# Plain products for the output projection and the values of an attention kernel with seven-product tricks, on one core

## The chip, the cores and the metric

The kernel runs on one core of one Trainium2 chip, all in float32 (the small feed-forward part in a split float32 form). The metric is the device time of one execution in microseconds, lower is better. The engines are named as in the profile: PE is TensorE's matmul, PEld its weight load, DVE VectorE, ACT ScalarE, POOL GpSimd, SP SyncE. SP, ACT and POOL also issue DMA transfers.

## The reference

`x` is 2048 x 256, there are 16 heads of 128, and a feed-forward of width 704 with weights rounded to -1, 0 and 1.

```python
xn = _layernorm(x, axis=-1)
# attention
qkv = einsum('bsd,ed->bse', xn, Wqkv).reshape(B, S, 3 * H, D)
q, k, v = qkv[:, :, :H], qkv[:, :, H:2*H], qkv[:, :, 2*H:]
w = softmax(einsum('bqhd,bkhd->bhqk', q, k) * D ** -0.5, axis=-1)
attn = einsum('bhqk,bkhd->bqhd', w, v).reshape(B, S, H * D)
attn = einsum('bse,de->bsd', attn, Wout)
# feed-forward on the same xn, weights quantized by their mean magnitude
ffn = bitlinear(sigmoid(bitlinear(xn, w1)) * bitlinear(xn, w2), w3)
return x + attn + ffn
```

## The kernel before, in words

**Blocks, tiles, groups.** After a lead-in (normalization, the feed-forward, the first head's Q, K and V) the kernel runs 64 blocks: 16 heads by 4 blocks of 512 queries. Two heads make a group (`G = 2`), so a group has 8 blocks, called block 0 to 7 of the group below; the last group is handled apart. A block has 4 tiles of 128 queries. The main loop has one step `u` per tile; the order of all instructions is written out by hand, and each engine takes its own in that order. `n` and `t` are the block and tile of the step.

**One step.** PE computes the scores of the tile six steps ahead (`scores`, `LEAD = 6`): 128 queries by 2048 keys, in two halves of 1024, out of three PSUM buffers. DVE takes the maximum of each half (`mx`, L630) and the negated one of both (`nm`, L633); ACT takes the exponential into `p` (L640), with the sums of rows. `exchanged` sends `p` to `part` by 16 transfers of 64 KB (L659), ten issued by SP and six by ACT: 32-row bands change places. Two steps later DVE turns `part` in 32x32 blocks into a slot of `R` (`transposed`, L706); now keys lie on partitions. The weighted sum of values is done by seven half-size products in place of eight (a Strassen-Winograd scheme over two halves of keys and two of head columns). It needs differences of `R` slots, taken by POOL (`differences`, L726: T1a and T3a in tile 3 of the block before; T1b, T3b and half of T2, called T2l, in tile 0; T2h and T4 in tile 1), and sums of V, taken by POOL once a head (`v_combined`, L748, two in tile 3 and two in tile 0 of a head's first block, which is block 0 or 4). `weighted` (L773) are these products, into `av`. Tile 1 needs T1, then T2l for its first half and T2h for its second. ACT copies and DVE adds quarters of `av` into `oU` (`copied` L791, `added` L799).

**The end of a block.** `inverses` (tile 2) makes 1/sum for the next block: a reduction, a reciprocal and a 32x32 turn on DVE, then four POOL-issued transfers of 4 x 32 numbers to DRAM (`rds`, L678). `spread` (tile 1 of that block) brings them back, the same on all partitions, into `oT` (L685). After tile 3 DVE multiplies `oU` by `oT` into `oT` (L801) and `put_away` sends `oT` to DRAM (`ods`, L827) at the start of the next block.

**Side products.** Each step also carries products that prepare other heads, through one PSUM bank `m` (`ps_m`, one buffer). `product(..., False)` runs right behind the scores; DVE reads its result behind `nm`; a second one (`twice`) follows the weighted products of the step, when the first has been read, and DVE reads it at the start of the next step (`left`). All are seven-product schemes, in 128x128x512 products cut into two 64-column halves (`in_halves`):
- tiles 2 and 3: Q and K of the next head, read by `fast_read`; in even blocks DVE also scales `kT` into `qT` (`fast_scaled`, L223), at the start of tile 3, and the first read of tile 3 (L197) needs that.
- tiles 0 and 1 of blocks 0 to 3: output projection of the group before (`fast_o_product`, `fast_o_read` L911), 7 products for two blocks, out of fetched pieces `o3` and their differences (POOL, L842), added into `osums`; running sums go to and from DRAM (`y_moved`, L839).
- tiles 0 and 1 of blocks 4 to 7: V of the next group (`fast_v_product`, `fast_v_read` L308 and L315), 7 products for half of the tokens. They give V with head columns on partitions, so it is sent to DRAM by bands (`v_sent`, L322), fetched (`v_landed`, L326) and turned by DVE (`v_transposed`, L331).

`between(n, t)` places all the POOL-issued transfers and sums at the end of a step. `weights[g, "v"]` and `weights[g, "o"]` share a buffer; their sums for the schemes (`sums_of`, L272 to L275) are POOL's.

Of the kernel before, what the change touches and what calls it, by code (L numbers as in the profile page):

```python
# [20 lines left out]
def layernorm_attention_bitffn_kernel(  # L21
# [197 lines left out]
    def fast_scaled(h: int, b: int):  # L219
        c = b // 2 * 2  # L220
        k1 = kTs[h].rearrange("p (j k r) -> p k j r", j=P // 32, r=32)[:, (c + 1) * TB : (c + 2) * TB]
        q0 = qTs[h, c].rearrange("p (k j r) -> p k j r", j=P // 32, r=32)
        nc.vector.tensor_scalar(q0, k1, SCALE, None, ALU.mult)  # L223
# [4 lines left out]
    o3 = const.tile([P, 3, QB], F32, tag="o3", name="o3")  # L228
# [36 lines left out]
    def v_sums(g: int):  # L265
        wv = weights[g, "v"]
        sums_of(wv[:, :, D:], wv[:, :, :D], f"wvs{g}")

    def sums_of(k, q, name: str):

        w = wpool.tile([P, 4, D], F32, tag="wx", name=name)
        nc.gpsimd.tensor_tensor(w[:, 0], q[:, 0], q[:, 1], ALU.add)  # L272
        nc.gpsimd.tensor_tensor(w[:, 1], w[:, 0], k[:, 0], ALU.subtract)
        nc.gpsimd.tensor_tensor(w[:, 2], k[:, 0], q[:, 0], ALU.subtract)
        nc.gpsimd.tensor_tensor(w[:, 3], k[:, 1], w[:, 1], ALU.subtract)  # L275
        wxs[name] = w


    def fast_v_product(g: int, m: int, second: bool):
        half, m = divmod(m, NB)  # L280
        wv, w, t = weights[g, "v"], wxs[f"wvs{g}"], ts[2 * half]
        x00, x10 = (xnT[:, d, bass.ts(2 * half, QB)] for d in range(KC))
        x11 = xnT[:, 1, bass.ts(2 * half + 1, QB)]
        lhs, rhs = (
            ((wv[:, 0, D:], x00), (w[:, 1], t[:, 1])),
            ((w[:, 2], t[:, 2]), (wv[:, 1, :D], t[:, 3])),
            ((w[:, 0], t[:, 0]), (w[:, 3], x11)),
            ((wv[:, 1, D:], x10),),
        )[m][second]
        pm = ps_m.tile([P, QB], F32, tag="m", name=f"pvw{g}_{half}_{m}_{int(second)}")  # L290
        in_halves(pm, lhs, rhs, True, True)
        return pm

    def v_half(h: int, half: int):
        return v_tile(h)[:, half * NKT // 2 : (half + 1) * NKT // 2]

    def fast_v_read(g: int, m: int, second: bool, pm):
        half, m = divmod(m, NB)
        q, k = (
            v_half(g * G + i, half).rearrange("p k d -> p (k d)").rearrange(  # L300
                "p (j k r) -> p k j r", j=P // 32, r=32
            )
            for i in range(G)
        )
        k0, k1, q0, q1 = k[:, :TB], k[:, TB:], q[:, :TB], q[:, TB:]
        pm = pm.rearrange("p (k j r) -> p k j r", j=P // 32, r=32)
        if (m, second) == (0, False):
            nc.vector.tensor_copy(k0, pm)  # L308
            return
        todo = {  # L310
            (0, True): ((k1, k0),), (1, False): ((q1, k1),), (1, True): ((q0, q1),),
            (2, False): ((q1, q1), (k1, k1)), (2, True): ((k1, k1),), (3, False): ((k0, k0),),
        }[m, second]
        for o, i in todo:
            nc.vector.tensor_tensor(o, pm, i, ALU.add)  # L315

    def v_sent(h: int, half: int):

        v = v_half(h, half).rearrange("p k d -> p (k d)")
        vd = vds[half].rearrange("(j r) (q c) -> q r j c", r=32, c=S // 8)  # L320
        for q in range(P // 32):
            nc.gpsimd.dma_start(vd[q], v[bass.ts(q, 32)].rearrange("r (j c) -> r j c", c=S // 8))  # L322

    def v_landed(half: int):
        for u in range(2):
            nc.gpsimd.dma_start(v_part[u], vds[half][:, bass.ts(u, QB)])  # L326

    def v_transposed(h: int, half: int):
        v = v_half(h, half).rearrange("p k (q r) -> p q k r", r=32)
        for u in range(2):  # L330
            nc.vector.transpose(  # L331
                v[:, 2 * u : 2 * u + 2], v_part[u].rearrange("p (q k r) -> p q k r", q=2, r=32)
            )

    wxs, v_part = {}, [xnT[:, 0, bass.ts(c, QB)] for c in (1, 3)]

# [11 lines left out]
        [away.tile([P, QB], F32, tag=f"od{h}_{c}", name=f"od{h}_{c}") for c in range(NB)]  # L348
        for h in range(2 * G)
    ]  # L350
    vds = [away.tile([P, S // 2], F32, tag=f"vd{i}", name=f"vd{i}") for i in range(2)]
    rds = [away.tile([TB, P], F32, tag=f"rd{i}", name=f"rd{i}") for i in range(2)]
# [311 lines left out]
    def inverses(n: int):  # L664
# [12 lines left out]
        for j in range(P // 32):  # L677
            nc.gpsimd.dma_start(  # L678
                rds[n % 2][:, bass.ts(j, 32)], riT[32 * j : 32 * j + TB, :]
            )  # L680

    def spread(n: int):

        if n < NBK - NB:
            nc.gpsimd.dma_start(oT, rds[n % 2].rearrange("t p -> (t p)").partition_broadcast(P))  # L685
            rbs[n] = oT
# [106 lines left out]
    def added(n: int, r: int):  # L793
# [6 lines left out]
        if r == 3 and n < NBK - NB:  # L800
            nc.vector.tensor_tensor(oT, u, rbs[n], ALU.mult)  # L801
# [22 lines left out]
    def put_away(n: int):  # L824

        h, b = blocks[n]
        nc.gpsimd.dma_start(ods[h % (2 * G)][b], oT)  # L827
# [6 lines left out]
    def o_fetched(g: int, pair: int, i: int, head: int, c: int):  # L834
        nc.gpsimd.dma_start(o3[:, i], ods[(g * G + head) % (2 * G)][2 * pair + c])

    def y_moved(pair: int, c: int, back: bool):
        y, yd = osums[:, c], yds[2 * pair + c]
        nc.gpsimd.dma_start(*((yd, y) if back else (y, yd)))  # L839

    def o_difference(i: int, a: int, b: int):
        nc.gpsimd.tensor_tensor(o3[:, i], o3[:, a], o3[:, b], ALU.subtract)  # L842

    def o_loaded(g: int, i: int):
        if i % 2 == 0:
            y_moved(i // 2, 0, False)

    def o_moved(g: int, i: int, t: int):

        pair, more = i // 2, i == 1  # L850
        at = i % 2, t
        if at == (0, 0):
            o_difference(1, 2, 1)
        elif at == (0, 1):
            o_difference(0, 1, 0)
        elif at == (0, 2):
            o_fetched(g, pair, 2, 1, 0)
        elif at == (1, 0):
            o_difference(2, 2, 1)
            if more:  # L860
                o_fetched(g, 1, 0, 0, 0)
        elif at == (1, 1):
            y_moved(pair, 1, True)
        elif at == (1, 2):
            if more:
                y_moved(1, 1, False)
                o_fetched(g, 1, 1, 0, 1)
            else:
                y_moved(pair, 0, True)
        elif at == (1, 3) and more:  # L870
            y_moved(pair, 0, True)
            o_fetched(g, 1, 2, 1, 1)
            o_difference(1, 1, 0)

    def o_begun(g: int, i: int, t: int):

        at = i, t
        if at == (6, 2):
            o_fetched(g, 0, 0, 0, 0)
        elif at == (6, 3):  # L880
            o_fetched(g, 0, 1, 0, 1)
        elif at == (7, 1):
            o_difference(1, 1, 0)
        elif at == (7, 2):
            o_fetched(g, 0, 2, 1, 1)

        if at == ((6, 3) if g else (7, 2)):
            y_moved(0, 1, False)

    def o_parts(g: int, m: int):  # L890
        w = weights[g, "o"]
        k, q = w[:, :, :P], w[:, :, P:]
        s = wxs[f"wos{g}"]
        k0, k1, q0, q1 = (0, 0), (1, 0), (0, 1), (1, 1)
        return (
            ((s[:, 0], 1, (k1, q1)), (s[:, 3], 2, (k1,))),
            ((k[:, 0], 0, (k1, q1, k0, q0)),),
            ((s[:, 2], 0, (q0, q1)), (k[:, 1], 2, (k0,))),
            ((s[:, 1], 1, (k1, q0, q1)), (q[:, 1], 2, (q0,))),
        )[m % NB]  # L900

    def fast_o_product(g: int, m: int, second: bool):
        lhs, i, _ = o_parts(g, m)[second]
        pm = ps_m.tile([P, QB], F32, tag="m", name=f"pow{g}_{m}_{int(second)}")
        in_halves(pm, lhs, o3[:, i], True, True)
        return pm

    def fast_o_read(g: int, m: int, second: bool, pm):
        for c, e in o_parts(g, m)[second][2]:
            y = osums[:, c, e]  # L910
            nc.vector.tensor_tensor(y, pm, y, ALU.add)  # L911

# [75 lines left out]
    def between(n: int, t: int):  # L988
# [3 lines left out]

        how = {
            (5, 0): (v_sent, 0, 0), (5, 2): (v_transposed, 0, 0), (6, 1): (v_transposed, 1, 0),
            (7, 0): (v_sent, 0, 1), (7, 2): (v_transposed, 0, 1),
        }.get((i, t))
        if t == 1:
            spread(n)
            if i == NB - 1 and g + 1 < H // G:
# [5 lines left out]
        elif n < last:  # L1005
            o_begun(g, i, t)
# [196 lines left out]
```

## Time and profile before

| | |
|---|---|
| time, median of 3 runs | 2299.64 us (2299.03 to 2301.24) |
| the profiled execution | 2299.23 us, span 2297.5 us |
| granted TensorE clock | 0.992 |
| DMA | 398.46 MB, mean 173 GB/s; 66% or so of 16 engines busy |
| mean of one: R difference L726, half / whole slot | 2.38 / 4.55 us |
| scaling L223 / multiplication L801 / addition L911 | 1.46 / 0.80 / 0.68 us |
| POOL issue of a transfer, L678 / L322 / L827 | 0.53 / 0.57 / 0.58 us |

A group line of the profile reads: line, engine, operation, written tile <- read tiles, shapes, count, then busy time, mean of one in ns, and the idle time before it with what ended it. The granted clock is the share of TensorE's clock that the throttle let through. Engines' busy times overlap; what counts is which of them is waited for.

### The profile page before, as it was taken

How to read it: one execution, taken by the hardware profiler on the slowest of the kernel's cores; microseconds unless marked ns; L12 is line 12 of the kernel's file. 1: busy time of each engine (PE TensorE's matmuls, PEld its weight loads, DVE VectorE, ACT ScalarE, POOL GpSimd, SP SyncE). 2: the span in 40 equal slices, each digit the busy share in tenths (PEclk: the TensorE clock that was granted, in tenths of full speed). 3: DMA queues.
4: the chain of work that ended last, by engine and by line, in shares of the span. 5: the costliest groups of instructions: out<-in, count | busy, mean ns of one | idle time of the engine just before them, and what ended most of it. 6: DMA issues, size and time to landing. Idle time of an engine off the chain costs nothing.

```text
span 2297.5 us, 41411 instructions
## 1 busy us (share of the span) xinstructions
PE 2189.6 (95%) x13514; PEld 1094.3 (48%) x13514; DVE 1887.3 (82%) x2562; ACT 744.9 (32%) x1390; POOL 1765.6 (77%) x1376
## 2 busy tenths in 40 slices
PE   9999999999999999899998999999999999999898
PEld 6744444454445444455444544444444544445455
DVE  6577888888788888789888888888888788888764
ACT  5543332333232323323333233332333233323331
POOL 0167878887788887988788887888789788898773
PEclk9999999999999999999999999999999999999999
DMA  2166667676676767776677766767677676776764
GB/s 89 55 151 155 150 179 196 166 208 158 175 205 173 189 161 190 193 193 184 162 184 187 199 175 174 198 173 191 159 183 210 171 185 161 189 194 184 193 172 123
DMA packets 246568, 398.46 MB, mean 173 GB/s; under 512 B 80720, under 2 KB 85264, under 8 KB 246352
## 3 DMA queue, kind: packets, MB, share of 16 engines
q1 hardware_dynamic: 127664, 174.95, 29.9%
q0 software_dynamic: 43792, 118.93, 18.6%
q10 hardware_dynamic: 74896, 101.94, 17.3%
q8 instruction: 106, 1.74, 0.3%
q14 instruction: 110, 0.90, 0.1%
HBM read 77.66 MB, written 49.41 MB: 55 GB/s over the span
## 4 chain that ended last, share of the span: by engine, by line
PE 28%; POOL 23%; DMA 19%; DVE 14%; issue 7%; SPq 5%; ACT 2%; ACTq 2%; DVEq 0%; POOLq 0%
DMA part<-p 17%; POOL R L726 14%; PE s L94 10%; PE av L773 8%; SPq L659 5%; DVE mx L630 4%; DVE R L706 3%; POOL st L748 2%; PE ph L508 2%; ACTq L659 2%; ACT p L640 2%; PE pow L94 1%; DVE oU L799 1%; PE pvw L94 1%; PE pw L94 1%
## 5 line engine op out<-in xcount | busy, mean ns | idle before, releaser
L726 POOL TENSOR_TENSOR R<-R 128x1024 f32<-128x1024 f32 x441 | 1181.6, 2686 | 37.0 <-DVE R L706 17.1
L640 ACT ACTIVATE p<-s,nm 128x1024 f32<-128x1024 f32 x512 | 566.2, 1111 | 1381.8 <-DMA part<-p 924.0
L94 PE MATMUL s<-kT,qT 128*64 128x512 f32 x4000 | 946.2, 594 | 13.9 <-ACT p L640 13.7
L630 DVE TENSOR_REDUCE mx<-s 128x1 f32<-128x1024 f32 x512 | 613.1, 1218 | 182.3 <-PE s L94 168.1
L706 DVE STREAM_TRANSPOSE R<-part 128x1024 f32<-128x1024 f32 x512 | 605.2, 1220 | 48.4 <-DMA part<-p 44.9
L94 PEld LDWEIGHTS s<-kT,qT 128*64 128x64 f32 x4000 | 331.1, 137 | 529.0 <-issue 442.1
L773 PE MATMUL av<-R,st 128*64 128x256 f32 x3024 | 495.9, 388 | 53.7 <-POOL R L726 50.2
L773 PE MATMUL av<-R,v 128*64 128x256 f32 x3728 | 539.7, 379 | 0.4 <-DVE oU L799 0.3
L773 PEld LDWEIGHTS av<-R,v 128*64 128x64 f32 x3728 | 341.9, 137 | 186.5 <-issue 56.7
L773 PEld LDWEIGHTS av<-R,st 128*64 128x64 f32 x3024 | 297.7, 139 | 208.1 <-POOL R L726 77.4
L678 POOL DMA_DIRECT2D rd<-r x240 | 124.8, 527 | 162.4 <-DVE r L676 162.1
L827 POOL DMA_DIRECT2D od<-oT x60 | 34.5, 575 | 157.7 <-DVE oT L801 150.2
L799 DVE TENSOR_TENSOR oU<-av,oU 64x256 f32<-64x256 f32 x248 | 101.1, 408 | 54.5 <-ACT oU L791 51.9
L911 DVE TENSOR_TENSOR osums<-pow,osums 128x512 f32<-128x512 f32 x196 | 124.6, 677 | 0.6 <-PE pow L94 0.6
L791 ACT COPY oU<-av 64x256 f32<-64x256 f32 x248 | 91.0, 367 | 94.4 <-PE av L773 90.1
L94 PE MATMUL pw<-t,ws 128*64 128x512 f32 x336 | 109.2, 592 | 0.0
L640 ACT ACTIVATION_READ_ACCUMULATOR p<-s,nm 128x1 f32 x512 | 100.2, 196 | 0.0
L160 POOL TENSOR_TENSOR t<-xnT 128x512 f32<-128x512 f32 x4 | 5.1, 1270 | 107.2 <-DMA part<-p 107.2
L315 DVE TENSOR_TENSOR v<-pvw,v 128x512 f32<-128x512 f32 x98 | 65.1, 676 | 24.9 <-PE pvw L94 24.9
L94 PE MATMUL pw<-xnT,wk 128*64 128x512 f32 x224 | 67.5, 599 | 14.2 <-DVE kT L200 14.2
L200 DVE TENSOR_TENSOR kT<-pw,kT 128x512 f32<-128x512 f32 x112 | 76.9, 686 | 1.8
L842 POOL TENSOR_TENSOR o<-o 128x512 f32<-128x512 f32 x56 | 71.7, 1280 | 0.5
(165 smaller groups left out, 1630.8 us busy)
## 6 DMA issues: line engine op xcount, KB each, us to landing
part<-p SPq DMA_DIRECT2D x2556, 64.0 KB, 2.2
part<-p ACTq DMA_DIRECT2D x1540, 64.0 KB, 2.5
oT<-rd POOLq DMA_DIRECT2D x60, 256.0 KB, 4.3
od<-oT POOLq DMA_DIRECT2D x60, 256.0 KB, 3.6
o<-od POOLq DMA_DIRECT2D x60, 256.0 KB, 4.4
vd<-v POOLq DMA_DIRECT2D x112, 128.0 KB, 3.6
xnT<-vd POOLq DMA_DIRECT2D x56, 256.0 KB, 5.2
osums<-yd POOLq DMA_DIRECT2D x28, 512.0 KB, 6.2
```

The source lines that it names most:

```text
L94: nc.tensor.matmul(out[c * HP : (c + 1) * HP], lhs[:, c * HP : (c + 1) * HP], rhs, start=start, stop=stop, skip_group_check=True,)
L200: nc.vector.tensor_tensor(k, pk, base, ALU.add)
L630: nc.vector.tensor_reduce(mx[:, i : i + 1], s, AX.X, ALU.max)
L640: nc.scalar.activation(p, s, AF.Exp, bias=nm, accum_out=sums[n][:, t, i : i + 1],)
L659: queue.dma_start(parts[v][g // 2][bass.ts(j, 32), g % 2, :], ps[j // 2][bass.ts(g, 32), bass.ts(j % 2, S // NQ)],)
L678: nc.gpsimd.dma_start(rds[n % 2][:, bass.ts(j, 32)], riT[32 * j : 32 * j + TB, :])
L706: nc.vector.transpose(to[:, t % 2, 2 * i : 2 * i + 2], part.rearrange("p g (s c) -> p g s c", s=2),)
L726: nc.gpsimd.tensor_tensor(o, x, y, ALU.subtract)
L773: nc.tensor.matmul(av[i * HP : (i + 1) * HP, half], l[:, kk], moving(s, kk), start=start, stop=(k == units[r] - 1), skip_group_check=True,)
L791: nc.scalar.copy(u[op, oq], av[ap, half])
L799: nc.vector.tensor_tensor(u[p, q], av[p, half], u[p, q], ALU.add)
L911: nc.vector.tensor_tensor(y, pm, y, ALU.add)
```

## The change

The output projection is done by plain products: for each block, two output halves by two heads, summed in PSUM (`o_product`), from one fetch of both heads' outputs, which now lie side by side in DRAM (`ods[g][b]`), with one read by DVE for each half (`o_read`). There are no differences of `o3` and no sums of `wo`. The running sums are loaded for the next block in tile 0 and stored in tile 2, and the next `o3` is fetched in tile 2.

The values of all groups are done by plain products with tokens on partitions (`v_product`), read by two DVE copies (`v_read`), as the lead-in does for the first group. The exchange of V through DRAM, its turning on DVE and the sums of `wv` are gone.

The reciprocals go to DRAM in one transfer of the whole 128 x 32 tile, and come back with another order of the columns, in pieces of 128 numbers; the multiplication by them follows that order, in place in `oU`, and `oU` itself is put away. The scaling of `fast_scaled` moves from DVE to ACT.

```diff
@@ fast_scaled
-        nc.vector.tensor_scalar(q0, k1, SCALE, None, ALU.mult)
+        nc.scalar.activation(q0, k1, AF.Copy, scale=SCALE)
...
-    o3 = const.tile([P, 3, QB], F32, tag="o3", name="o3")
+    o3 = const.tile([P, G, QB], F32, tag="o3", name="o3")
...
-    (v_sums, sums_of, fast_v_product, v_half, fast_v_read, v_sent, v_landed, v_transposed)
+    def v_product(g: int, m: int, second: bool):
+        w = weights[g, "v"]
+        pm = ps_m.tile([P, 2, G * D], F32, tag="m", name=f"pvw{g}_{m}")
+        for j in range(2):
+            for d in range(KC):
+                in_halves(
+                    pm[:, j], xnT[:, d, bass.ts(2 * m + j, P)], w[:, d], d == 0, d == KC - 1
+                )
         return pm
+    def v_read(g: int, m: int, second: bool, pm):
+        for j in range(G):
+            nc.vector.tensor_copy(
+                v_tile(g * G + j)[:, 2 * m : 2 * m + 2], pm[:, :, bass.ts(j, D)]
+            )
...
     ods = [
-        [away.tile([P, QB], F32, tag=f"od{h}_{c}", name=f"od{h}_{c}") for c in range(NB)]
-        for h in range(2 * G)
+        [away.tile([P, G, QB], F32, tag=f"od{g}_{c}", name=f"od{g}_{c}") for c in range(NB)]
+        for g in range(2)
     ]
-    rds = [away.tile([TB, P], F32, tag=f"rd{i}", name=f"rd{i}") for i in range(2)]
+    rds = [away.tile([P, 32], F32, tag=f"rd{i}", name=f"rd{i}") for i in range(2)]
@@ inverses, spread
-        for j in range(P // 32):
-            nc.gpsimd.dma_start(
-                rds[n % 2][:, bass.ts(j, 32)], riT[32 * j : 32 * j + TB, :]
-            )
+        nc.gpsimd.dma_start(rds[n % 2], riT)
...
-            nc.gpsimd.dma_start(oT, rds[n % 2].rearrange("t p -> (t p)").partition_broadcast(P))
+            r = rds[n % 2].rearrange("(j c) r -> j (c r)", c=32)[:, : TB * 32]
+            nc.gpsimd.dma_start(
+                oT.rearrange("p (j x) -> p j x", j=P // 32), r.partition_broadcast(P)
+            )
@@ added
-            nc.vector.tensor_tensor(oT, u, rbs[n], ALU.mult)
+            u = u.rearrange("p (t j r) -> p t j r", t=TB, r=32)
+            r = rbs[n].rearrange("p (j t r) -> p t j r", t=TB, r=32)
+            nc.vector.tensor_tensor(u, u, r, ALU.mult)
@@ put_away
-        nc.gpsimd.dma_start(ods[h % (2 * G)][b], oT)
+        nc.gpsimd.dma_start(ods[h // G % 2][b][:, h % G], oU)
...
-    (o_difference, o_loaded, o_moved, o_begun, o_parts, fast_o_product, fast_o_read)
+    def o_fetched(g: int, b: int):
+        nc.gpsimd.dma_start(o3, ods[g % 2][b])
+    def y_moved(b: int, back: bool):
+        y, yd = osums[:, (b + 1) % 2], yds[b]
         nc.gpsimd.dma_start(*((yd, y) if back else (y, yd)))
+    def o_product(g: int, m: int, second: bool):
         w = weights[g, "o"]
+        pm = ps_m.tile([P, QB], F32, tag="m", name=f"pow{g}_{m}")
+        for i in range(G):
+            in_halves(pm, w[:, i, bass.ts(m % 2, P)], o3[:, i], i == 0, i == G - 1)
         return pm
+    def o_read(g: int, m: int, second: bool, pm):
+        y = osums[:, (m // 2 + 1) % 2, m % 2]
+        nc.vector.tensor_tensor(y, pm, y, ALU.add)
@@ between
         if g and i < NB:
-            o_moved(g - 1, i, t)
-        elif n < last:
-            o_begun(g, i, t)
+            if t == 0 and i + 1 < NB:
+                y_moved(i + 1, False)
+            elif t == 2:
+                y_moved(i, True)
+                if i + 1 < NB:
+                    o_fetched(g - 1, i + 1)
+        elif n < last and (i, t) == (GB - 1, 2):
+            y_moved(0, False)
+            o_fetched(g, 0)
...
@@ main loop
-                    product, read, twice = fast_o_product, fast_o_read, j % NB != 1
+                    product, read, twice = o_product, o_read, False
...
-                    product, read, twice = fast_v_product, fast_v_read, j % NB != NB - 1
+                    product, read, twice = v_product, v_read, False
```

All calls of the removed functions in `between` and in the main loop are gone too.

More of the change, by code (lines that the diff above doesn't have):

```diff
@@ L259, in v_place @@
         return (k + NKT // 2) % NKT if h == 1 else k
[L265 to L276, printed above, removed]
@@ L279, in fast_v_product @@
[L279 to L291, printed above, removed]
-        return pm
@@ L294, in v_half @@
[L294 to L301, printed above, removed]
-            )
-            for i in range(G)
-        )
[L305 to L333, printed above, removed]
@@ L335, in layernorm_attention_bitffn_kernel @@
-    wxs, v_part = {}, [xnT[:, 0, bass.ts(c, QB)] for c in (1, 3)]
+    def v_product(g: int, m: int, second: bool):
[6 more added lines that the diff above has]
+                )
+        return pm
+    def v_read(g: int, m: int, second: bool, pm):
+        for j in range(G):
+            nc.vector.tensor_copy(
+                v_tile(g * G + j)[:, 2 * m : 2 * m + 2], pm[:, :, bass.ts(j, D)]
+            )
@@ L347, in layernorm_attention_bitffn_kernel @@
     ods = [
-        [away.tile([P, QB], F32, tag=f"od{h}_{c}", name=f"od{h}_{c}") for c in range(NB)]
-        for h in range(2 * G)
-    ]
-    vds = [away.tile([P, S // 2], F32, tag=f"vd{i}", name=f"vd{i}") for i in range(2)]
-    rds = [away.tile([TB, P], F32, tag=f"rd{i}", name=f"rd{i}") for i in range(2)]
+        [away.tile([P, G, QB], F32, tag=f"od{g}_{c}", name=f"od{g}_{c}") for c in range(NB)]
+        for g in range(2)
+    ]
+    rds = [away.tile([P, 32], F32, tag=f"rd{i}", name=f"rd{i}") for i in range(2)]
     def loads(fraw):
@@ L676, in inverses @@
         nc.vector.transpose(riT, ri)
-        for j in range(P // 32):
-            nc.gpsimd.dma_start(
-                rds[n % 2][:, bass.ts(j, 32)], riT[32 * j : 32 * j + TB, :]
-            )
+        nc.gpsimd.dma_start(rds[n % 2], riT)
     def spread(n: int):
         if n < NBK - NB:
-            nc.gpsimd.dma_start(oT, rds[n % 2].rearrange("t p -> (t p)").partition_broadcast(P))
+            r = rds[n % 2].rearrange("(j c) r -> j (c r)", c=32)[:, : TB * 32]
+            nc.gpsimd.dma_start(
+                oT.rearrange("p (j x) -> p j x", j=P // 32), r.partition_broadcast(P)
+            )
             rbs[n] = oT
@@ L826, in put_away @@
         h, b = blocks[n]
-        nc.gpsimd.dma_start(ods[h % (2 * G)][b], oT)
[L834 to L838, printed above, removed]
-        nc.gpsimd.dma_start(*((yd, y) if back else (y, yd)))
-    def o_difference(i: int, a: int, b: int):
-        nc.gpsimd.tensor_tensor(o3[:, i], o3[:, a], o3[:, b], ALU.subtract)
@@ L844, in o_loaded @@
[L844 to L890, printed above, removed]
-        w = weights[g, "o"]
[L892 to L905, printed above, removed]
-        return pm
[L908 to L911, printed above, removed]
+        nc.gpsimd.dma_start(ods[h // G % 2][b][:, h % G], oU)
@@ L991, in between @@
         last = NBK - NB
[L993 to L996, printed above, removed]
         if t == 1:
@@ L1003, in between @@
         if g and i < NB:
-            o_moved(g - 1, i, t)
-        elif n < last:
-            o_begun(g, i, t)
-        if i in (5, 7) and t % 2 and g + 1 < H // G:
-            v_landed(i // 2 - 2)
-        if how and g + 1 < H // G:
-            how[0]((g + 1) * G + how[1], how[2])
+            if t == 0 and i + 1 < NB:
[7 more added lines that the diff above has]
+            o_fetched(g, 0)
         if n >= last - 1 and t == (1 if n < last else 2):
             b = n + 1 - last
-            nc.gpsimd.dma_start(o3[:, b % 2], ods[(H - 2) % (2 * G)][b])
-        if g and (i, t) == (0, 1):
-            v_transposed(g * G + 1, 1)
-        if t == 2:
-            if i == GB - 1 and n < last:
-                wo = weights[g, "o"]
-                sums_of(wo[:, :, :P], wo[:, :, P:], f"wos{g}")
-            if i in (5, 7) and g + 1 < H // G:
-                v_sent((g + 1) * G + 1, i // 2 - 2)
-        if t == 3:
-            if i == NB - 1 and g + 1 < H // G:
-                v_sums(g + 1)
+            nc.gpsimd.dma_start(o3[:, b % 2], ods[(H - 2) // G % 2][b][:, 0])
         if t == 2 and last - 1 <= n < last + NB - 1:
@@ L1069, in layernorm_attention_bitffn_kernel @@
                     put_away(n - 1)
-                if n >= GB and n % GB < NB:
-                    o_loaded(n // GB - 1, n % GB)
                 differences(n, "T1b")
```

## The prediction

> **What bounds the kernel now.** I read the page's first part, the chain of waits, a table of windows cut at block starts, the waits of PE and the timelines of single engines, in that order.
>
> ```profile
> PE 2189.6 (95%) x13514; PEld 1094.3 (48%) x13514; DVE 1887.3 (82%) x2562; ACT 744.9 (32%) x1390; POOL 1765.6 (77%) x1376
> ```
>
> PE leads, DVE and POOL are close behind. A busy PE need not be a fast PE, so I looked for its full rate in the chain:
>
> ```profile
> 1055.92 3.45 PE av L773 x32
> 1059.37 0.86 PE pow L94 x4
> 1060.23 3.43 PE s L94 x16
> ```
>
> A record is one of two passes over one 64-column half. A plain product of 128x128x512 is four records: 0.86 us. The four score products of a tile take 3.43. A weighted product has a moving side of 256 columns, 32 records take 3.45, 0.108 each, half of the 0.214 of a 512-wide one. From these I make a floor for a block: scores 4 x 3.43 = 13.7; weighted products 112 records x 0.108 = 12.1; then 0.86 for each side product (Q/K of the next head, V of the next group or output projection of the last), of which block 0 to 3 of a group have 7, blocks 4 and 6 have 8, blocks 5 and 7 have 6. Floors: 31.8, 32.7 and 31.0.
>
> The windows of one group (block 0 to 7; length, then busy time of PE, PEld, DVE, ACT, POOL, granted clock, DMA share and GB/s):
>
> ```profile
> 1217.90:1255.60 37.70, 33.11 (x206) 14.99 (x204) 33.06 (x43) 12.12 (x23) 33.67 (x24) 1.00 0.66 170
> 1255.60:1287.50 31.90, 31.90 (x207) 19.32 (x205) 28.61 (x41) 9.94 (x19) 25.44 (x19) 1.00 0.71 198
> 1287.50:1321.90 34.40, 33.37 (x208) 17.09 (x205) 30.57 (x40) 10.99 (x22) 30.92 (x26) 1.00 0.71 195
> 1321.90:1354.00 32.10, 31.98 (x206) 17.23 (x204) 28.62 (x41) 9.65 (x20) 24.93 (x18) 1.00 0.67 185
> 1354.00:1389.50 35.50, 33.68 (x213) 16.19 (x210) 28.27 (x37) 12.18 (x23) 28.86 (x21) 1.00 0.61 149
> 1389.50:1421.80 32.30, 31.76 (x204) 14.51 (x202) 27.50 (x39) 9.33 (x19) 26.14 (x23) 1.00 0.76 186
> 1421.80:1455.10 33.30, 33.09 (x210) 14.74 (x208) 30.20 (x40) 11.96 (x23) 27.59 (x23) 1.00 0.69 174
> 1455.10:1488.10 33.00, 31.74 (x202) 14.53 (x200) 27.41 (x39) 9.36 (x19) 29.19 (x29) 1.00 0.84 226
> ```
>
> Blocks 1 and 3 run at the floor. Above it stand 5.9 (block 0), 2.6 (2), 2.8 (4), 1.3 (5), 0.6 (6) and 2.0 (7): 15.6 in this group. The timeline has the first score of block 8 at 400.5 and of block 56 at 2033.0, so a group lasts 272.1 on average and stands 17.6 above its floor of 254.5. What makes these 17.6:
>
> ```profile
> PE av L773 <- POOL R L726: 50.2, 41, 4.1
> PE pw L94 <- DVE kT L200: 14.2, 13, 3.1
> PE s L94 <- ACT p L640: 13.7, 11, 6.1
> PE pow L94 <- DVE osums L911: 5.0, 9, 0.6
> ```
>
> (Who waited for whom: us, times, longest. [...]) POOL's differences are late at a head's first block, DVE's reads hold the single PSUM bank `m`, and ACT's exponentials are late now and then.
>
> **The change, part by part.**
>
> *PE.* The projection goes from 14 to 16 products a group, 2 x 0.86 = 1.7 more. V goes from 14 products 512 wide to 64 half products 256 wide, two records each: 128 x 0.108 = 13.8 against 12.0, 1.7 more. Each is done seven times: 7 x 3.43 = **+24 us**, bare, since PE is the engine at its floor. It falls in blocks 0, 2, 5 and 7. [...] The rows show the 256-wide stream at exactly half, with a weight load at each, so I keep 13.8.
>
> *POOL.* Gone: 180 reciprocal transfers x 0.52 = 94, the 56 `o` differences 72, 168 issues of V's exchange 94, the sums of `wv` and `wo` 29, half of the 56 `o` fetches 16: 305 of 1766. Most of it lay beside PE. Bare was what stands ahead of `R` at a head's first block. In block 0 POOL issues `od` at 1223.74 after two `xnT<-vd`, then runs a y load, T1b and T3b, two V sums, T2l, an `o` difference and T2h, and PE waits 1.4 and 1.6 for T2l and T2h at 1234.47 and 1238.02. After the change: `od` 0.57, T1b and T3b 4.81, V sums 2.54, T2l 2.34, y load 0.55, T2h 2.34 = 13.2 after DVE's multiplication. That ends 5.3 after the block's start now, 4.0 in block 4 and 2.5 in unhurried blocks; without V's work ahead of it on DVE I take 3.3, between the last two, so T2h ends at 16.5. PE needs it at two scores 6.86, two side products 3.43, the weighted product of tile 0 3.45 and half of the next 1.73 = 15.5: 1.0 left of a wait. In block 4 `od` would now wait for DVE, whose multiplication ends at 1358.04 and not for POOL (1358.71): T2h at 4.0 + 12.6 = 16.6, 1.1 left of 2.8.
>
> *DVE.* Gone: transposes of V 37, 140 of 196 additions to `osums` 89, the scaling 41; V's reads go from 74.6 to 112 copies of 256 at 0.43 (row of L820) = 48. That is 194 of 1887. The 14.2 of `pw` behind `kT`, in blocks 5 and 7, comes from V's transposes that wait for `xnT<-vd`: gone. So is the wait of second `pow` and `pvw` products for the first's read, since all of a step's products now share one bank and one read. The multiplication by 1/sum keeps its size (0.69 alone, 1.69 at most); runs of 32 could cost nothing or bring it to the 1.6 of the scaling's row, whose views have such runs; I take 0.7.
>
> *ACT.* 28 scalings at 0.60 (row of L132) are 17 us at 32% busy, but the place counts:
>
> ```profile
> 1247.45 6.32 ACTq L659 DMA_DIRECT2D part<-p  x6
> 1254.15 1.11 ACT L640 ACTIVATE p<-s,nm 128x1024 f32<-128x1024 f32 x1 [6.92 <-DVE nm L633]
> ```
>
> ```profile
> 1250.01 1.61 DVE L223 TENSOR_SCALAR qT<-kT 128x512 f32<-128x512 f32 x1
> 1251.54 2.34 DVE L630 TENSOR_REDUCE mx<-s 128x1 f32<-128x1024 f32 x2
> 1253.99 0.68 DVE L197 SCALAR_TENSOR_TENSOR qT<-pw,qT 128x512 f32<-128x512 f32 x1
> ```
>
> This is tile 3 of block 0, begun at 1248.0. DVE's 1.6 leaves and L197 could start at 5.1 after the start in place of 6.0; but now it waits for the scaling, which stands behind ACT's six `part` issues (end 5.8 here; 3.5 to 4.7 in block 4). Behind L197 on DVE are the transposes and the addition, behind it on PE the second Q product, wanted at 6.0. Blocks 4 and 6 gain 0.5; in 0 and 2 it depends on the queue below.
>
> *oU put away.* ACT's first copy of a block (L791, 8.1 after its start, 8.9 with a longer product ahead) now waits for the landing of `od` from the same tile: issue at 2.8, 3.6 to land (2.7 to 6.0), so 6.4 to 8.8: hidden. If the issue is late as in block 0 (5.8), up to 2.9 on ACT, with its `part` issues and exponentials behind; POOL's relief puts it at 4, so I take 0.3.
>
> *DMA.* 29 of 398 MB go. The broadcast in pieces of 512 B and the one `rd` have a block's time; nothing. But at tile 2 of blocks 0, 1 and 2 a y store and an `o` fetch of 512 KB each now follow `rd` at once; today there is one fetch of 256 KB (0, 2) or 768 KB some 1.5 us later (1). A y load lands in 6.2, a y store in 4.7. A transfer then delays the `part` landings that ACT's later issues wait for: ACT's issues end at 5.8 after 256 KB, at 4.4 to 7.5 after 768, at 8.5 in block 7 (1218.24, tile begun at 1209.7) after 1 MB and more. I take 6.0, near the two closest rows, and keep 8.5 as the bad end. Then scaling and L197 end at 7.2 and PE loses 1.2 in blocks 0 and 2 (0.5 now).
>
> **The sum.** Time above the floor after: block 0 2.7 to 3.3, block 1 0.6, block 2 2.0, block 3 0.5, block 4 1.2, blocks 5 and 6 0.4 each, block 7 0.7: about 9, and 10 for the average group (scaled by 17.6/15.6). 17.6 - 10 = 7.6 won, 3.4 paid: 4.2 a group, seven times 29. From 2299.2 (the profiled time; the median is 0.4 higher) to **2270**. The tail has one burst less at block 59 (2 us), which I leave in the range.
>
> **The rivals.**
>
> *The bursts land on ACT (slower).* ACT's issues end at 8.5 at tile 3 of blocks 0, 1, 2: L197 ends at 9.7, 3.7 late in 0 and 2; exponentials start late enough to hold the next scores by about 1.9 in blocks 1 and 7. That is 8 more a group than forecast: 18 above the floor, 3.4 + 0.4 a group worse, 2326. It decides from 4.2 more, an issue end of about 7.2. For it: the 11.4 us that ACT waited at block 59 behind 2.8 MB. Against it: block 1 bears 768 KB with no loss of its own. I put its times at 2305 to 2326. 16%.
>
> *Nearly everything won.* PE is left with the head-change waits, 1 in blocks 0 and 4, and 2 elsewhere: 4 above the floor, 7 x (3.4 - 13.6) = -71, 2228; half way from the forecast, 2248. For it: DVE and POOL lose 194 and 305 us at once. Against it: block 4 has almost no V work and still loses 2.8. 17%.
>
> *Even.* 14 stay: the relief only moves POOL's waiting to `od`, which waited 150 us for DVE already. 2295 to 2304. 8%.
>
> **How the numbers follow.** The forecast (2255 to 2295 of its own) holds 59%. A measurement of this kernel tells about 0.2%, 4.6 us. Faster by more: 59 + 17 = 76%; within: 8%; slower: 16%. The range goes from 2238, into the good rival, to 2308, into the bad one, and leaves out some 9% on either side.
>
> **What would show it.** Blocks 1 and 3 stay near 31.8; block 0 is at 35 to 36, block 4 at 34; V's 16 records of a step take 1.7; PE's wait for `R` falls from 50 to about 20; `pw <- kT` goes; POOL falls below 1500 busy. Wrong if V's records stand further apart than 0.108, if ACT's `part` issues at tile 3 of blocks 0 to 2 end after 7.2, or if PE's waits for ACT grow past 40.

## The result and the profile after

The changed kernel takes 2310.28 us (median of six runs, 2303.37 to 2313.47), the kernel before 2299.34 beside it: a ratio of 1.0043, interval 1.0027 to 1.006. It is slower by some 11 us, 0.4%, where 29 less were forecast, and 2310 lies just outside the stated range, which ended at 2308. The profiled execution took 2310.64 us, its span is 2308.9.

The page's first part: PE busier by the products added, DVE and POOL relieved by 173 and 288 us, and yet a longer span.

```profile
PE 2202.1 (95%) x14074; PEld 1223.0 (53%) x14074; DVE 1714.1 (74%) x2338; ACT 760.1 (33%) x1418; POOL 1477.6 (64%) x888
```

The windows of one group, cut at block starts (columns as before):

```profile
1212.70:1252.40 39.70, 34.16 (x211) 15.45 (x209) 26.48 (x34) 12.94 (x24) 26.92 (x17) 1.00 0.68 175
1252.40:1284.30 31.90, 31.90 (x208) 14.69 (x206) 25.62 (x35) 8.90 (x18) 22.91 (x14) 1.00 0.74 191
1284.30:1326.40 42.10, 34.52 (x210) 15.29 (x208) 27.35 (x35) 13.80 (x26) 24.53 (x18) 0.96 0.66 173
1326.40:1359.80 33.40, 33.40 (x208) 14.75 (x206) 25.40 (x35) 8.04 (x16) 22.17 (x13) 0.95 0.62 153
1359.80:1394.40 34.60, 33.46 (x226) 16.43 (x224) 26.05 (x36) 12.76 (x24) 25.04 (x14) 1.00 0.63 150
1394.40:1426.30 31.90, 31.90 (x223) 22.41 (x220) 25.90 (x38) 9.85 (x19) 20.48 (x10) 1.00 0.62 145
1426.30:1459.10 32.80, 32.80 (x228) 23.13 (x226) 26.50 (x36) 12.25 (x24) 22.18 (x14) 1.00 0.65 152
1459.10:1490.90 31.80, 31.80 (x222) 24.17 (x220) 25.86 (x38) 9.06 (x18) 22.48 (x14) 1.00 0.68 172
```

Blocks 5, 6 and 7 run at their new floors. With the projection's two products more, the floor of blocks 0 and 2 is 32.7: block 0 stands 7.0 above it, block 2 (in this group the worst of all) 9.4, and block 3, in which PE is never idle, loses 1.6 to a granted clock of 0.95. Over six groups (blocks 8 to 55, from the first scores of each in the timelines) the mean lengths are:

| kernel | 0 | 1 | 2 | 3 | 4 | 5 | 6 | 7 | group |
|---|---|---|---|---|---|---|---|---|---|
| before | 38.10 | 31.83 | 34.74 | 31.92 | 35.41 | 32.87 | 33.49 | 33.73 | 272.1 |
| after | 39.38 | 32.06 | 38.86 | 32.49 | 34.60 | 31.85 | 32.73 | 31.85 | 273.8 |

The half of the group with the values won 4.5, the half with the projection lost 6.2. PE's waits say by what:

```profile
PE s L94 <- ACT p L582: 37.7, 23, 4.1
PE pw L94 <- DVE qT L197: 29.6, 13, 5.8
PE av L715 <- POOL R L668: 22.3, 31, 3.0
PE pw L94 <- DVE kT L200: 1.5, 1, 1.5
```

The waits for POOL's `R` fell from 50.2 to 22.3 and those for `kT` from 14.2 to 1.5, as forecast. (`pw` is bank `m` in the products for Q and K, `pow` in those of the projection, `pvw` in those of the values; a row says which engine waited for which result.) Those for ACT's exponentials rose from 13.7 to 37.7, and the wait for `qT` is now 29.6; in the kernel before it was

```profile
PE pw L94 <- DVE qT L197: 1.1, 4, 0.6
```

Both come of tile 3. Over the same six groups the wait for `qT` stands in tile 3 of blocks 0 and 2 (1.5 and 3.1 a group), the one for the exponentials in the tile that follows: tile 0 of block 0, behind block 7 of the group before (2.1 a group), and tile 0 of block 2, behind block 1 (1.8). In block 2 of the group above, tile 3 begins at 1312.2 (timelines of ACT, DVE and PE; L601 is the `part` issue, L223 the scaling, L582 the exponential, L197 the read of Q):

```profile
1314.55 8.64 ACTq L601 DMA_DIRECT2D part<-p  x6
1323.24 0.63 ACT L223 ACTIVATE qT<-kT 128x512 f32<-128x512 f32 x1 [8.89 <-DMA part<-p]
1323.78 1.10 ACT L582 ACTIVATE p<-s,nm 128x1024 f32<-128x1024 f32 x1
1323.90 0.69 DVE L197 SCALAR_TENSOR_TENSOR qT<-pw,qT 128x512 f32<-128x512 f32 x1 [6.20 <-ACT qT L223]
1324.65 1.98 PE L94 MATMUL pw<-t,wq 128*64 128x512 f32 x4 [5.81 <-DVE qT L197]
```

ACT spends 8.64 us on six issues, the scaling and the exponential stand behind them, DVE's read waits 6.20 for the scaling, and PE 5.81 for the bank that this read frees. The reason lies in the DMA engines. The same stretch in windows of 2 us:

```profile
1314.00:1316.00 2.00, 2.00 (x12) 0.65 (x10) 1.48 (x2) 0.34 (x2) 1.92 (x2) 1.00 1.04 376
1316.00:1318.00 2.00, 2.00 (x17) 1.14 (x15) 1.38 (x2) 0.00 (x0) 1.74 (x1) 1.00 1.04 249
1318.00:1320.00 2.00, 0.83 (x6) 0.27 (x2) 0.00 (x0) 0.00 (x0) 0.00 (x0) 1.00 0.72 142
1320.00:1322.00 2.00, 0.00 (x0) 0.00 (x0) 0.00 (x0) 0.00 (x0) 0.00 (x0) 1.00 0.17 43
1322.00:1324.00 2.00, 0.00 (x0) 0.00 (x0) 0.10 (x1) 0.76 (x2) 0.00 (x0) 0.65 0.73 173
1324.00:1326.00 2.00, 1.35 (x4) 0.53 (x6) 2.00 (x3) 2.00 (x4) 0.00 (x0) 0.50 0.52 122
1326.00:1328.00 2.00, 2.00 (x6) 0.47 (x4) 1.93 (x3) 0.42 (x2) 0.00 (x0) 0.50 0.58 136
```

(A transfer has landed when its completion is signalled.) POOL issued the y store at 1311.06 and the `o` fetch at 1311.59. All 16 engines are full from 1314 to 1318 (share 1.04); the fetch lands at 1320.24, and the eight `part` pieces that SP and ACT had issued from 1314.03 to 1316.70 land only behind it, from 1320.44 to 1321.67: 4.9 to 6.4 us after their issue, where the median piece takes 2.1 (SP) and 2.2 (ACT). ACT's fourth issue begins at 1321.19, SP's sixth at 1320.46; until then nothing new goes out, hence the share of 0.17.

Why the issues stop there can be read in the trace. All DMA transfers that SP and ACT issue signal the same eight semaphores, in this kernel and in the one before, and in neither did any of the 4112 issues begin before the last transfer on its semaphore had landed: eight are under way at most. Here the eight were five of SP and three of ACT, and all landed behind the fetch. SP's sixth issue uses the semaphore of the piece that landed at 1320.44, ACT's fourth that of SP's third piece, which landed at 1321.16. So ACT's queue stood for landings of its own and of SP's pieces, and those for the fetch.

The last column but two is the granted clock: at 0.50 after the wait. I come back to it.

Over the six groups ACT's issues of tile 3 end at these times after its start (mean, lowest to highest):

| | block 0 | block 1 | block 2 | block 7 |
|---|---|---|---|---|
| before | 5.3 (4.5 to 5.8) | 5.6 (4.4 to 7.5) | 5.9 (5.6 to 6.4) | 7.9 (5.8 to 9.7) |
| after | 6.7 (6.1 to 7.7) | 8.3 (7.5 to 8.9) | 8.2 (5.0 to 11.0) | 8.8 (8.0 to 9.8) |

The 5.0 is block 26, where POOL came 1.5 us later to the two transfers than in the other groups; PE shows no wait for `qT` there. Block 7 issues 1 MB in tile 2 too: the y load and the `o` fetch for the next group.

### The profile page after: what moved, and what is told of

Its sections match the earlier page's. It is cut to its first block, busy times and chain, and to the rows that moved or that the text cites. A ratio compares the mean times of both kernels' runs of the same rounds, so it can differ in the third digit from the quotient of the medians.

```text
span 2308.9 us, 41828 instructions
## 1 busy us (share of the span) xinstructions
PE 2202.1 (95%) x14074; PEld 1223.0 (53%) x14074; DVE 1714.1 (74%) x2338; ACT 760.1 (33%) x1418; POOL 1477.6 (64%) x888
## 3 DMA queue, kind: packets, MB, share of 16 engines
q0 software_dynamic: 27728, 90.39, 15.9%
HBM read 62.98 MB, written 35.59 MB: 43 GB/s over the span
## 5 line engine op out<-in xcount | busy, mean ns | idle before, releaser
L94 PE MATMUL s<-kT,qT 128*64 128x512 f32 x4000 | 960.2, 598 | 37.7 <-ACT p L582 37.7
L582 ACT ACTIVATE p<-s,nm 128x1024 f32<-128x1024 f32 x512 | 565.5, 1109 | 1155.3 <-DMA part<-p 706.1
L572 DVE TENSOR_REDUCE mx<-s 128x1 f32<-128x1024 f32 x512 | 620.6, 1222 | 321.1 <-PE s L94 307.8
L94 PEld LDWEIGHTS s<-kT,qT 128*64 128x64 f32 x4000 | 382.6, 138 | 479.0 <-issue 283.0
L715 PE MATMUL av<-R,st 128*64 128x256 f32 x3024 | 485.5, 384 | 27.3 <-POOL R L668 22.3
L771 POOL DMA_DIRECT2D od<-oU x60 | 34.2, 569 | 299.2 <-DVE oU L745 294.8
L619 POOL DMA_DIRECT2D rd<-r x60 | 33.5, 559 | 248.1 <-DVE r L618 248.1
L94 PE MATMUL pvw<-wv,xnT 128*64 128x256 f32 x896 | 116.2, 379 | 0.0
L94 PE MATMUL pow<-o,wo 128*64 128x512 f32 x448 | 107.6, 601 | 0.0
L582 ACT ACTIVATION_READ_ACCUMULATOR p<-s,nm 128x1 f32 x512 | 100.3, 196 | 0.0
L94 PEld LDWEIGHTS pvw<-wv,xnT 128*64 128x64 f32 x896 | 80.1, 137 | 37.4 <-issue 8.0
L197 DVE SCALAR_TENSOR_TENSOR qT<-pw,qT 128x512 f32<-128x512 f32 x84 | 57.8, 688 | 35.1 <-ACT qT L223 34.3
```

The costliest lines, as they stand in the source:

```text
L94: nc.tensor.matmul(out[c * HP : (c + 1) * HP], lhs[:, c * HP : (c + 1) * HP], rhs, start=start, stop=stop, skip_group_check=True,)
L197: nc.vector.scalar_tensor_tensor(q, pm, SCALE, base, ALU.mult, ALU.add)
L572: nc.vector.tensor_reduce(mx[:, i : i + 1], s, AX.X, ALU.max)
L582: nc.scalar.activation(p, s, AF.Exp, bias=nm, accum_out=sums[n][:, t, i : i + 1],)
L619: nc.gpsimd.dma_start(rds[n % 2], riT)
L715: nc.tensor.matmul(av[i * HP : (i + 1) * HP, half], l[:, kk], moving(s, kk), start=start, stop=(k == units[r] - 1), skip_group_check=True,)
```

## The experiments

**Undo one part of the changed kernel, or take its cost away.** Four kernels tell apart the place of the scaling, the place of the transfers, and their bytes.

The scaling back on DVE:

```diff
-        nc.scalar.activation(q0, k1, AF.Copy, scale=SCALE)
+        nc.vector.tensor_scalar(q0, k1, SCALE, None, ALU.mult)
```

> The changed kernel with the scaling of qT back on DVE, nothing else. What the changed kernel shows: PE's second Q product at tile 3 waits for DVE's L197, that for ACT's scaling, that stands behind six part issues which end 6 to 11 us after the tile's start in blocks 0 and 2. Theory A (the scaling's place on ACT is the cost): the waits of pw for qT, 34 us by the sum of PE's lost time, fall to about 0.5 us a block; since the exponentials stay late, some of it comes back as scores waiting for p at tile 0 of blocks 1 and 3; 2285 to 2297. Theory B (the transfers at tile 2 are the cost and the scaling only shows it first): the same time goes over to scores waiting for p, 2303 to 2312.

Measured: 2290.49 us (2284.58 to 2296.72), 0.996 of the kernel before, run beside it (95% interval 0.9945 to 0.9976; written so in brackets from here on). PE's waits:

```profile
PE s L94 <- ACT p L582: 37.7, 28, 4.8
...
PE pow L94 <- DVE qT L197: 13.5, 12, 1.5
...
PE pw L94 <- DVE qT L197: 2.2, 3, 1.5
```

The wait of `pw` for `qT` fell from 29.6 to 2.2, but 13.5 came in its place one step later, where the projection's first product of blocks 1 and 3 waits for DVE's second read of tile 3: about half of the wait is won. The wait for the exponentials stayed. So some 19 of the changed kernel's us (0.996 against 1.0043) are the scaling's place behind the issues, part of them through the granted clock (below); the late issues go on to cost through the exponentials.

The same move in the kernel before (its line is the one above, the other way round):

> The kernel before with the scaling of qT on ACT, nothing else. ACT's part issues end there 5.2 to 6.4 us after the start of tile 3 in blocks 0 and 2 and 3.5 to 5.8 in 4 and 6; L197 started at 6.0. Theory A: L197 at 6.4 to 7.0 in blocks 0 and 2 (0.7 us lost each), 5.4 in 4 and 6 (0.5 won each), so within 3 us of the kernel before; a loss appears only together with the later end of the issues. If ACT is the wrong place by itself: 2305 or more.

Measured: 2296.8 us, 0.9997 [0.9983, 1.0012]. Without the two transfers at tile 2, ACT is as good a place as DVE. Taken with the experiment above, the move costs only together with the late issues.

The y store and the `o` fetch one tile earlier in the changed kernel:

```diff
-            elif t == 2:
+            elif t == 1:
                 y_moved(i, True)
```

> The changed kernel with the y store and the next o fetch (512 KB each) issued at the end of tile 1 instead of tile 2, some 7 us earlier. Theory B (what costs is that 1 MB lands among the part transfers of tile 2, which ACT issues then, before the short tile 3): ACT's part issues at tile 3 of blocks 0 to 2 end at 4 to 6 us instead of 6 to 11, the waits of pw for qT and of scores for p shrink to a third, 2262 to 2285. Rival (1 MB costs wherever it is put, through the DMA engines' share): the wait goes to tile 2, 2300 to 2312. Theory A alone expects 2303 to 2312, too.

Measured: 2308.28 us, 1.0046 [1.0029, 1.0064]. A miss for theory B, and inside the range of its rivals. Block 1's issues ended at 6.7 instead of 8.3, block 0's at 6.7 as in the changed kernel, and block 2's at 9.8, later than the changed kernel's 8.2, since POOL lagged there by most of a tile and issued the fetch only 2.4 us ahead of tile 3. The waits for `qT` stayed in tile 3. The order in the program did not settle when the bytes moved, so whether 1 MB would be harmless at another place stays open.

The bytes themselves: the y stores of blocks 0 to 2 and the `o` fetches of blocks 1 to 3 move 64 of 512 columns, so a part of the projection's sums is neither stored nor fetched.

```diff
-        nc.gpsimd.dma_start(o3, ods[g % 2][b])
+        c = slice(0, QB if b == 0 else QB // 8)
+        nc.gpsimd.dma_start(o3[:, :, c], ods[g % 2][b][:, :, c])
...
+        if back and b < NB - 1:
+            y, yd = y[:, :, : QB // 8], yd[:, :, : QB // 8]
```

> The changed kernel with the y store of blocks 0 to 2 and the o fetches for blocks 1 to 3 cut to an eighth of their columns (64 KB each), issued at the same places; part of the projection's sums is thus not stored or fetched. It bounds what the bytes at tile 2 cost. Theory B: blocks 0 and 2 lose 2 waits each of 2 to 5 us, some 7 us a group, 2250 to 2268. If the changed broadcast (512 pieces in place of 128) or the scaling's place is the cost by itself, it stays above 2295.

Measured: 2245.57 us (2244.06 to 2248.38), 0.9775 [0.9756, 0.9793]. ACT's issues end at 4.1, 5.8 and 4.9 in blocks 0 to 2, and the waits are:

```profile
PE av L715 <- POOL R L668: 22.5, 34, 3.4
PE s L94 <- ACT p L582: 17.6, 12, 3.6
```

The wait for `qT` is down to 0.9, with the scaling still on ACT. Seven eighths of the bytes of 21 stores and 21 fetches thus cost the changed kernel some 62 us (0.9775 against 1.0043), the 19 of the scaling among them: about 3 us a pair. Of the 17.6 that are left for the exponentials, 9.7 stand in tile 0 of block 0 (six groups), behind block 7, whose 1 MB was left whole.

**One part of the change alone, in the kernel before.** The plain values (the diff's `v_product` and `v_read`, without the exchange):

> The kernel before with the values of all groups by plain products, nothing else (projection, reciprocals and scaling as before). In the changed kernel blocks 4 to 7, where V is made, take 34.4 + 31.9 + 32.7 + 31.9 = 130.8 us a group against 134.4 before, though PE has 1.7 us more to do. If the parts add up: 3.6 us won there and 1 to 2 in block 0, where V's exchange still ran, seven times: 2258 to 2270. Rival (the clean V blocks of the changed kernel owe it to the single reciprocal transfer and the lighter POOL, not to V): 2280 to 2298.

Measured: 2269.86 us (2268.09 to 2271.63), 0.9863 [0.9845, 0.9881], at the slow end of the theory's range and outside the rival's. That it is also the time that the prediction gave to the whole change is chance.

The plain projection (the diff's `o_product`, `o_read`, `o_fetched` and `y_moved`), with its transfers at tile 2:

> The kernel before with the projection by plain products alone: V's exchange, reciprocals and scaling as before. Theory (what the change lost, it lost in blocks 0 to 3 by the 1 MB at tile 2): the V blocks stay as before or get worse at tile 3 of block 7, where 1 MB now joins V's exchange; 4 to 6 us a group lost in blocks 0 to 3, 2315 to 2335. With the scaling on DVE the loss shows as scores waiting for p. Rival (the projection is harmless without the scaling on ACT): 2295 to 2308.

Measured: 2320.49 us, 1.0083 [1.006, 1.0106]. This is in the theory's range and outside the rival's. Its bare price is 7 groups x 2 products x 0.86 = 12; blocks 1 to 3 grow by 0.8, 3.1 and 0.3. The loss shows as the exponentials, whose wait is 30.5 us where it was 13.7, most of it in tile 0 of block 2 (2.8 a group); ACT's issues of block 1 end at 9.8 there.

The reciprocals' part (the diff's lines in `inverses`, `spread`, `added` and `put_away`): one transfer, pieces of 512 B, the product in place in `oU`, `oU` put away.

> The kernel before with the reciprocals' part alone: one transfer of 16 KB to DRAM, the broadcast in 512 pieces of 512 B instead of 128 of 2 KB, the multiplication in place in oU and oU put away. In the changed kernel the broadcast lands in 5.7 us against 4.3. Theory: POOL's 1.55 us a block were spare and the landing has a block's time, 2292 to 2300. Rival (the pieces hold up part transfers, or ACT's first copy waits for oU to be put away): 2305 or more.

Measured: 2319.36 us, 1.0077 [1.0059, 1.0096]. A miss for the theory. By its mean blocks, block 0 won 3.1 and blocks 3, 5 and 7 lost 1.5, 1.0 and 3.7. In block 7 DVE turns V in program order ahead of reading `kT`; first the kernel before, then this one:

```profile
1482.65 1.30 DVE L331 STREAM_TRANSPOSE v<-xnT 128x512 f32<-128x512 f32 x2 [1.30 <-DMA rd<-r]
```

```profile
1504.67 0.71 DVE L331 STREAM_TRANSPOSE v<-xnT 128x512 f32<-128x512 f32 x1 [3.34 <-DMA xnT<-vd]
```

The spreading takes 6.0 instead of 4.3 us, and the two fetches of V that POOL issues behind it land 7.1 and 7.8 us after their issue instead of 5.3 and 5.4.

The same without the pieces (four transfers to DRAM, spread in 2 KB; `oU` still in place), against the kernel just shown:

```diff
-        nc.gpsimd.dma_start(rds[n % 2], riT)
+        for j in range(P // 32):
+            nc.gpsimd.dma_start(
+                rds[n % 2][:, bass.ts(j, 32)], riT[32 * j : 32 * j + TB, :]
+            )
...
```

The shape of `rds`, `spread` and the order of the columns in the multiplication go back with it.

> The kernel before with only this of the change: the product with the reciprocals in place in oU, and oU put away. The reciprocals go to DRAM in four transfers and are spread in pieces of 2 KB, as in the kernel before. Theory A: the 17 us that the whole part cost alone came from the pieces of 512 B; the spreading took 6.0 us there instead of 4.3, POOL's queue lands in order, and the pieces of the values behind it landed 7.1 us after their issue instead of 5.3, so that DVE's copies of kT came late (PE waited 42.6 us for kT instead of 14.2). With 2 KB again the time is that of the kernel before within 0.4 % (2294 to 2312 beside 2303) and the wait for kT is 10 to 20 us. Theory B: it was the put away of oU, for which ACT's copies waited 8.0 us in all: the time stays over 2312.

Measured: 2297.82 us, 0.9991 [0.9975, 1.0008], the wait for `kT` at 12.4. Theory A holds so far as the two can be parted: the cost was the one transfer together with its pieces, and the put away of `oU` is free. And this edit in the changed kernel:

> The changed kernel with the reciprocals in four transfers and spread in pieces of 2 KB again; all else as changed. Theory A: the pieces of 512 B hold up what lies behind them in POOL's queue here too (the store of y and the fetch of o), so 5 to 15 us of the changed kernel's time are theirs: 2293 to 2306 where the kernel before takes 2300. Theory B: without the exchange of values nothing lies behind the spreading that anyone waits for, and three more issues of POOL at 0.52 us go against it: 2306 to 2316, no difference from the changed kernel that can be told.

Measured: 2306.75 us, 1.0042 [1.002, 1.0064], against 1.0043: no difference. With the exchange of V gone, nobody waits for what lies behind the pieces.

**Towards a better version.** The changed kernel with the scaling on DVE and the y store moved on to tile 3, the fetch left at tile 2:

```diff
-            elif t == 2:
+            elif t == 2 and i + 1 < NB:
+                o_fetched(g - 1, i + 1)
+            elif t == 3:
                 y_moved(i, True)
-                if i + 1 < NB:
-                    o_fetched(g - 1, i + 1)
```

> The changed kernel with the scaling on DVE (2290 alone) and the y store moved from tile 2 to the end of tile 3, so that 512 KB instead of 1 MB stand together at tile 2. Cutting the bytes to an eighth gave 2246. If the size of the burst decides: half of that comes back, 2262 to 2278. If the o fetch (6.9 us to land) does the harm alone: 2284 to 2292.

Measured: 2281.84 us, 0.9907 [0.989, 0.9924], between the two expectations. Parting the two transfers wins some 12 us more (0.9907 against 0.996). The exponentials wait less in tile 0 of block 2 (2.2 us in six groups for 6.0 with the scaling alone put back), but more in tile 0 of block 3 (7.0 for 5.5), behind the tile in which the store now goes out.

The plain values alone, and POOL's sums of `wo` out of the way of block 0:

```diff
+            if i == GB - 1 and n < last:
+                load_weights(g, "o", nc.gpsimd)
             spread(n)
...
-        if t == 2:
+        if t == 1:
             if i == GB - 1 and n < last:
                 wo = weights[g, "o"]
```

> The kernel before with the plain values alone, and POOL's four sums of the output weights (1.86 us) made in tile 1 of block 7, where POOL is idle for 4.6 us, instead of tile 2, ahead of the reciprocal products R that block 0 waits for; the weights are loaded ahead of the spreading for it. Theory A: POOL's backlog is what block 0 waits for (24.6 us at tile 1 and 6.9 at tile 0 over seven groups): up to 1.9 us a group are gained, 2256 to 2264 where the plain values alone took 2270 and the kernel before 2303. Theory B: POOL's store of oT waits for DVE at that place anyway, so nothing is gained: 2266 to 2274.

Measured: 2259.82 us, 0.9829 [0.9805, 0.9852]; theory A's gain, and block 0 is 0.9 shorter, 37.06 against 37.94. With the reciprocals' part of the change added:

> The kernel before with the plain values, the sums of the output weights made early, and the whole reciprocals part of the change (one transfer, pieces of 512 B, product in place in oU); the projection stays as before. Theory A: alone, that part cost 17 us only because the exchange of values lay behind the pieces in POOL's queue (blocks 5 and 7 lost 28 us more, blocks 2 and 3 some 13, while block 0 lost 18 us less, as POOL issues one transfer at tile 3 instead of four). Without that exchange the gain of block 0 is left, and part of the 13 us: 2245 to 2260 where the same kernel with the old reciprocals took 2260 and the kernel before 2299. Theory B: the pieces hold up the fetches of o, which POOL's differences and the projection wait for, as much as the issues gain: 2260 to 2272.

Measured: 2248.76 us (2247.45 to 2256.39), 0.9783 [0.9766, 0.98], in theory A's range and the fastest complete version. Block 0 goes from 37.06 to 35.59. So one edit cost 17 us in one kernel, nothing in a second, and won some 11 in a third. This version is also the change without its projection and with the scaling on DVE (and the sums of `wo`, which the old projection needs, made early): what it leaves out cost the changed kernel some 60 us (0.9783 against 1.0043), of which 12 are products.

## Why the prediction was wrong

**The failed step** is in the paragraph *DMA*: ACT's issues at tile 3 of blocks 0 to 2 were taken to end at 6.0, "near the two closest rows", with 8.5 as the bad end. They end at 6.7, 8.3 and 8.2, past the point of 7.2 from which the prediction let its first rival decide, in two blocks of three. The rows that it called closest (256 KB at once, or 768 KB 1.5 us later) are both short of the 1 MB at once that the change issues; the row of block 7, 1 MB and more, was nearer and gave 8.5. The bounds were right and the choice between them was wrong. From the 6.0 the sum took 1.2 us of loss at L197 in blocks 0 and 2 and nothing for late exponentials. PE's waits there are 1.5 and 3.1 us a group for L197, and 2.1 (tile 0 of block 0) and 1.8 (tile 0 of block 2) for exponentials. The first of these two stands behind block 7, where the sum had no charge at all for the 1 MB in tile 2: before, the same place waited 0.05 us a group. The rival's mechanism, the bursts landing on ACT's issues with scaling and exponentials behind, is what happened: the transfers' bytes cost some 62 us in all, 19 of them through the scaling.

**The rival's size** was 2326, its range 2305 to 2326, and 2310 lies in it. A group stands 15.9 above its floor (273.8 less 257.9) where the forecast had 10 and the rival 18. It charged 3.7 to L197 in blocks 0 and 2 alike, but block 0's issues end 1.5 earlier than block 2's. Its 1.9 for the exponentials behind blocks 1 and 7 came out at 1.8 and 2.1.

**Right.** PE's bare price: a V step of 16 records lasts 1.73 (the two starts below), 0.108 a record, as the rows of the kernel before had it. POOL's and DVE's relief was 288 and 173 us for 305 and 194. `pw` behind `kT` is gone, the wait for `R` is 22 for 20. Block 4 took 34.6 for 34, blocks 1 and 3 32.1 and 32.5. The put away of `oU` is hidden. "Nothing" for the pieces was right in the changed kernel, but not as a property of the pieces: with the exchange of V behind them they and the one transfer cost 17 us.

```profile
1363.70 1.90 PE L94 MATMUL pvw<-wv,xnT 128*64 128x256 f32 x16
1365.43 3.62 PE L715 MATMUL av<-R,v 128*64 128x256 f32 x32
```

**What came of it:** blocks 0 and 2 took 39.4 and 38.9 where 35 to 36 and 34.7 (2.0 above the floor) were forecast. Apart from that, the lead-in and the end together took 1.1 more, where a gain of 2 had been left in the range.

**Not in the sum at all:** the granted clock. Summed over windows between 250 and 2080 us of the profiled executions (length x (1 - granted clock)), the kernel before loses 6.8 us, the changed one 10.2, the projection alone 17.1, the reciprocals alone 20.5, and the scaling put back 3.4; the version with small moves and the fastest complete one lose none. One execution of each says little, since these losses come in steps of 1.7 (3.41 us at 0.50). Over all executions on record, span x (1 - granted clock) is on average 27 us for the changed kernel (six), 20 for the kernel before (72), 16 with the scaling put back (12) and 13 with small moves (4). By this estimate, which also counts half clock in which PE waits, some 7 of the 11 us, 11 of the 19 and 14 of the 62 are not the waits but what follows them.

How the four parts add up: alone they make -1.4, +0.8, 0.0 and +0.8 %, together +0.2 %, and the whole change made +0.4 %. That is no confirmation: the reciprocals cost nothing in it, and the scaling some 19 us. Each part's price belongs to what it shares a queue with.

What stays open is whether 1 MB could be issued anywhere in a block without such a loss: one tile earlier won nothing, and parting the two transfers won 12 of the 43 us that are left of the 62 when the scaling is put back.

## What to carry to other kernels

Before a small instruction is moved to an engine with idle time, read what stands ahead of it in that engine's order, and what those things wait for when the new traffic is there. Two transfers of 512 KB, issued in one go ahead of an exchange of small pieces that the next step waits for, cost this kernel about 3 us of its time a pair, though the DMA engines are busy for some two thirds of the time only (64%); cost a transfer by what lands behind it. When a change has several parts, build the parts: here one was worth some 32 us, and the others spent it. Measure a part in the kernel in which it is to stand: the reciprocals' part cost, did nothing and won in three of them.

## What the runs showed of the hardware

**Five of seven waits of PE were followed by half clock.** PE waited 5.81 us from 1318.8 on, and from 1322.6 to 1329.4 the clock was granted at 0.50. PE ran again from 1324.7, so 4.8 us of work went at half speed, about 2.4 us on top of the wait; that is the lower clock of blocks 2 and 3 above. Waits of 2.53 (at 670.7) and 4.00 us (at 774.7) were each followed by 3.41 us at 0.50, a loss of 1.7. Of seven waits over 2.5 us in blocks 8 to 57 of the changed kernel five were followed so; those of 2.89 (at 502.1) and 3.01 us (at 946.0) were not. Since 2.53 was enough once and 3.01 was not, length alone did not decide; what else did is left open. Between 250 and 2080 us the clock stood at 0.50 in five stretches in the changed kernel and in three in the kernel before, all of 3.41 us but one of 6.83 in each.

**64 KB pieces waited behind a transfer of 512 KB that another engine had issued.** In the stretch shown, the pieces of SP and ACT landed 4.9 to 6.4 us after their issue, all behind POOL's 512 KB. From 1314 to 1317, at a share of 1.03, POOL's queue moved 0.86 MB and those of SP and ACT together 0.22 MB: little of the small pieces came through, and none of the eight landed before the fetch. Over the 25 such fetches between 300 and 2060 us, 190 pieces were issued during one and more than 2.5 us before it landed. They took 5.6 us on average, and the 28 of them that landed ahead of it had all been issued within 1.2 us of it.

**With pieces of 512 B a spreading of 256 KB** lasted 6.0 us in the kernel with the reciprocals' part alone, where it took 4.3 with pieces of 2 KB in the kernel before (5.7 in the changed kernel, 4.3 with the pieces of 2 KB back), and the transfers behind it in POOL's order landed up to 2.4 us later (7.8 against 5.4). POOL's transfers landed in the order of their issue without exception: 685 in the kernel before, 309 in the changed one.
